# The conditioned part's weights and first x go into the first attention's memory, loaded while the last sample is still in work

## The chip, the cores and the metric

The kernel runs on one core of one Trainium2 chip. The metric is the device time of one execution in microseconds (us), lower is better. The core has five instruction queues that each work in order: PE (TensorE, matrix products and transposes; the loading of its weights is shown as PEld), DVE (VectorE), ACT (ScalarE), POOL (GpSimd) and SP (SyncE, which here only issues transfers). On-chip memory is SBUF, 128 partitions wide; products land in PSUM, which has eight banks. Inputs lie in DRAM and come in by DMA.

## The reference, cut to what matters

x has 16 samples of 256 tokens by 256 features, in float32. Four residual steps follow each other:

```python
x = x + attn0(cross_attention(x, fside, stage embedding))     # 16 heads of 16
x = x + fp4_feed_forward(x @ W[cat] + b[cat])                 # weights and rows quantized in blocks of 16
x = x + attn1(diffusion(x, zX, zY, zR))                       # 16 heads of 64, causal segments of 128
y = concat(gelu(x @ fc1.T + b1) @ fc2.T + b2,                 # 192 shared columns
           gelu(x @ fc1.T + b1) @ experts[idx].T + be[idx])   # 64 columns of the sample's own expert
x = x + SCALE * (shared_expert(y) + sum of the two best of eight experts(y), gated by softmax(y @ w_router))
```

The line that makes y is called the conditioned part here.

## The kernel before

`program` runs three things: `setup`, `woven` and `mixture`.

**woven** does the first three residual steps, one sample after another. It is a set of generators ("streams"): `stage_a` and `stage_e` (the cross attention and the first attention), `stage_f` (the quantized feed-forward), `stage_d`, `stage_p`, `stage_g` and `stage_v` (diffusion, projections, scores and values of the second attention), and some that prepare weights. `weave` asks each stream for its next operation, plans the time at which the operation could start (fixed costs per engine, 4.5 us for a transfer to land, 0.06 us for issuing one) and issues the earliest one. What it issues stands in that order on each engine (`tc.manual_schedule()`). Streams wait for each other through counters: `done["A"]` counts samples whose first attention is finished, `done["F"]` those whose feed-forward is. Samples overlap: while one is in the second attention, the next ones are in the first.

All of woven's operations carry line 162 in the profile (the helper that issues them), so they are told apart by their tiles: `wq`, `wv` and `wo` are weights of the second attention, loaded again for every group of four heads into two buffers each; `e_zT` is its normalized input; `f_ppT`, `f_oT` and `pmo` belong to its last product; `x` is the sample. When a sample is finished, `stage_v` stores it to DRAM (`xd<-x`). `stage_f` stores zeros to a DRAM table, two stores of 1 MB for each sample (`ysort<-zero`), right after the sample's feed-forward; the two of the last sample are woven's last ones.

woven's SBUF is divided into pools: `w` (weights), `x`, `sa` (all tiles of the cross attention and the first attention), `sf` (feed-forward) and `sl` (second attention). The pools are laid out one behind another and are all given back when woven ends.

**mixture** follows. Its pools lie where woven's were. It opens a PSUM pool of two times four banks (`bank0`, `bank1`), a pool `moe_keep` whose first tile is `xs` (all of x), and others, and calls `conditioned`, which loads its own weights in a pool `c2_w` (lines 1373 to 1400), then works through eight blocks of 512 tokens. A block loads the two samples' expert columns into `own` (line 1407), transposes x (line 107, then copies at line 113 into `g_xT`), and does 32 matmul instructions with `fc1` (each product of float32 data is two instructions), a gelu on ACT (line 1424), 16 with `fc2`, 32 with `own`, the router's logits and `route`, which scatters rows by indirect DMA from POOL. All matmuls of this part carry line 49, all loads of x line 1111. Unlike woven, this part is not in a written order: a list scheduler places each instruction on its engine when its own model of time finds it ready, later in the program or not. After `conditioned` come the tile plan (`plan_tiles`, line 1315 stores zeros to `osort`), four shared blocks, 35 or more tiles of the experts and the last four shared blocks.

Of the kernel before, what the change touches and what calls it, by code (L numbers as in the profile page):

```python
# [12 lines left out]
F32 = mybir.dt.float32  # L13
# [6 lines left out]
P = 128  # L20
S = 256
D = 256
# [5 lines left out]
FF1 = 1024  # L28
NE = 8
# [15 lines left out]
def mm(nc, out, pairs, start=True, stop=True):  # L45

    last = len(pairs) - 1
    for i, (lhsT, rhs) in enumerate(pairs):
        nc.tensor.matmul(out, lhsT, rhs, start=start and i == 0, stop=stop and i == last)  # L49
# [245 lines left out]
def woven(k):  # L295
    nc, tc = k.nc, k.tc
    with ExitStack() as ctx:
        g = Stages()
        g.k, g.a, g.B, g.ident = k, k.a, k.B, k.ident
        g.pe, g.dve, g.act = Unit("PE", nc.tensor), Unit("DVE", nc.vector), Unit("ACT", nc.scalar)  # L300
        g.pool, g.sp = Unit("POOL", nc.gpsimd), Unit("SP", nc.sync)
        pool = lambda name, bufs, **kw: ctx.enter_context(tc.tile_pool(name=name, bufs=bufs, **kw))
        g.w = pool("w", 1)
        g.xp = pool("x", 5)
        g.a_, g.f_, g.l_ = pool("sa", 1), pool("sf", 1), pool("sl", 1)
        space = bass.MemoryType.PSUM
        psum = pool("psum", 1, space=space)
        g.pairs = [psum.tile([P, 2, 512], F32, name=f"pair{i}") for i in range(PAIRS)]
        g.singles = [psum.tile([P, 512], F32, name=f"single{i}") for i in range(8 - 2 * PAIRS)]
        g.zT = {}  # L310
        g.live, g.kT = {}, {}
        g.x, g.io, g.done = {}, {}, {"W": 0, "D": 0, "Z": 0, "A": 0, "M": 0, "E": 0, "F": 0, "P": 0, "G": 0, "V": 0, "L": 0}
        with tc.manual_schedule():
            weave([stage_a(g), stage_e(g), stage_gate(g), stage_up(g), stage_down(g), stage_f(g), stage_g(g), stage_p(g), stage_d(g), stage_v(g), stage_fill(g)])
# [80 lines left out]
def stage_e(g):  # L395

    for b in range(g.B):
        o = g.a_.tile([P, 2, D], F32, name="b_o", tag="b_o")
        before = None
        for n in range(5):  # L400
            if n < 4:
                yield lambda: g.done["M"] > 4 * b + n
                kT, qS = g.kT.pop(4 * b + n), (yield from queries_transposed(g, n))
                prob = [(yield from heads_exponential(g, 0, kT, qS))]
            if n > 0:
                yield from heads_values(g, n - 1, before, o)
            if n < 4:
                prob.append((yield from heads_exponential(g, 2, kT, qS)))
                g.done["E"] += 1
            before = prob  # L410
        oT = g.a_.tile([P, 2, S], F32, name="b_oT", tag="b_oT")
        both = yield from single(g, o)
        pt = both.rearrange("p (c s) -> p c s", c=2)
        for c in range(2):
            for st in range(2):
                yield g.pe.transpose(pt[:, c, st * P : (st + 1) * P], o[:, st, c * P : (c + 1) * P], g.ident)
        yield copy_(g, oT, pt)
        g.singles.append(both)
        both = yield from single(g, oT)
        pp = both.rearrange("p (s d) -> p s d", s=2)  # L420
        for st in range(2):
            yield from mm_(g, pp[:, st, :], [(oT[:, c, st * P : (st + 1) * P], g.wout0[:, c, :]) for c in range(2)])
        yield g.dve.tensor_tensor(g.x[b], g.x[b], pp, ALU.add)
        g.singles.append(both)
        g.done["A"] = b + 1


def fetch_a(g, b):
# [530 lines left out]
def stage_g(g):  # L959

    for i in range(4 * g.B):
        yield lambda: g.done["P"] > i and g.done["V"] > i - 2
        g.live[i] = yield from scores4(g, i % 4, *g.live[i])
        g.done["G"] = i + 1
# [403 lines left out]
def conditioned(k, keep, r):  # L1368

    nc, tc, a = k.nc, k.tc, k.a  # L1370
    B, NT = k.B, 2 * k.B
    with ExitStack() as ctx:
        w = ctx.enter_context(tc.tile_pool(name="c2_w", bufs=1))
        p2 = ctx.enter_context(tc.tile_pool(name="c2_p2", bufs=2))

        def load(name, shape, src):
            t = w.tile(shape, F32, name=name)
            nc.sync.dma_start(out=t, in_=src)
            return t

        fc1 = load("fc1", [P, 2, FF1], a["fc1"])
        fc1b = load("fc1b", [P, 8], a["fc1b"])
        fc2 = load("fc2", [P, 8, P], a["fc2a"])
        fc2b = load("fc2b", [P, 1], a["fc2_b"][0:P].unsqueeze(1))

        wr = w.tile([P, 2, P + NE], F32, name="wr")
        nc.sync.dma_start(out=wr[:, :, P:], in_=a["w_router"])
        nc.vector.tensor_copy(wr[:, :, 0:P], k.ident.unsqueeze(1).to_broadcast([P, 2, P]))
        expb = load("expb", [16, 64], a["L1_cond2_experts_b"])

        bias2 = w.tile([P, B], F32, name="bias2")
        shared_b = load("shared_b", [64, 1], a["fc2_b"][P : P + 64].unsqueeze(1))
        nc.vector.tensor_copy(bias2[0:64, :], shared_b.to_broadcast([64, B]))
        pb = bank(k)
        mm(nc, pb[64:128, :B], [(expb, k.onehot[0:16, 2, :])])
        nc.vector.tensor_copy(bias2[64:128, :], pb[64:128, :B])
        own = []
        for i in range(3):
            t = w.tile([P, 8, P], F32, name=f"own{i}")
            nc.sync.dma_start(out=t[:, :, 0:64], in_=a["fc2c"])  # L1400
            own.append(t)

        for blk in range(NT // 4):
            k.stream = blk % 2
            for b in (2 * blk, 2 * blk + 1):
                which = nc.sync.value_load(k.idx[0:1, 2, b : b + 1], min_val=0, max_val=15)
                nc.sync.dma_start(
                    out=own[b % 3][:, :, 64:128], in_=a["exp_w"][bass.ds(which, 1)].rearrange("e p f m -> p (e f) m")
                )
                if b + 2 < B:  # L1410
                    load_x(k, b + 2)
            xT = p2.tile([P, 2, 512], F32, name="g_xT", tag="g_xT")
            transposed(
                k,
                xT.rearrange("p c (s t) -> p (c s) t", t=P),
                [k.xs[:, 4 * blk + s, c * P : (c + 1) * P] for c in range(2) for s in range(4)],
            )
            x = k.xs[:, 4 * blk : 4 * blk + 4, :]
            nc.gpsimd.tensor_tensor(x, x, k.bs2.unsqueeze(1).to_broadcast([P, 4, D]), ALU.add)
            hT = k.hp.tile([P, 8, 512], F32, name="hT", tag="hT")  # L1420
            for f in range(8):
                ph = bank(k)
                mm(nc, ph, [(fc1[:, c, f * P : (f + 1) * P], xT[:, c, :]) for c in range(2)])
                nc.scalar.activation(hT[:, f, :], ph, AF.Gelu, bias=fc1b[:, f : f + 1])
            py = bank(k)
            mm(nc, py, [(fc2[:, f, :], hT[:, f, :]) for f in range(8)])
            nc.vector.tensor_scalar(k.yT[:, 0, blk * 512 : (blk + 1) * 512], py, fc2b, None, ALU.add)
            for i in range(2):
                b = 2 * blk + i
                py = bank(k)[:, :S]  # L1430
                mm(nc, py, [(own[b % 3][:, f, :], hT[:, f, i * S : (i + 1) * S]) for f in range(8)])
                nc.vector.tensor_scalar(k.yT[:, 1, b * S : (b + 1) * S], py, bias2[:, b : b + 1], None, ALU.add)

            logits = p2.tile([P, 4, NE], F32, name="logits", tag="logits")
            part = p2.tile([P, 4, NE], F32, name="part", tag="part")
            ys = []
            for t4 in range(4):
                tok = slice(blk * 512 + t4 * P, blk * 512 + (t4 + 1) * P)
                py = bank(k)[:, : 2 * (P + NE)].rearrange("p (c w) -> p c w", c=2)
                for c in range(2):  # L1440
                    mm(nc, py[:, c, :], [(k.yT[:, c, tok], wr[:, c, :])])
                nc.vector.tensor_copy(part[:, t4, :], py[:, 1, P:])
                nc.vector.tensor_tensor(logits[:, t4, :], py[:, 0, P:], part[:, t4, :], ALU.add)
                y = p2.tile([P, 2, P], F32, name="r_y", tag="r_y", bufs=5)
                copies(k)(y, py[:, :, 0:P])
                ys.append(y.rearrange("p c d -> p (c d)"))
            route(k, r, p2, logits, ys, 4 * blk, 4)


def program(tc, a, out, n_batch):  # L1450
# [102 lines left out]
```

## Time and profile before

| what | value |
|---|---|
| median of 3 runs | 2787.61 us (2787.22 to 2788.68) |
| the profiled execution's own time | 2794.98 us |
| span of the profiled execution, first to last instruction | 2793.3 us |
| PE busy | 2701.6 us, 97% of the span |
| DVE, ACT, POOL busy | 1434.2, 934.3, 856.5 us |
| mean granted PE clock | 0.977 |
| last first-attention product on PE (`wout,b_oT`) starts | 1602.3 us |
| last feed-forward product group into x (`downT,d_hT`) starts on PE | 1667.9 us |
| woven's last PE product ends | 1799.9 us |
| first `fc1` product of the conditioned part | 1814.49 us |
| conditioned part's last router product | about 2064 us |

The profile gives times in microseconds from the span's start. A row of the timeline has the start, the length, the engine (SPq is a transfer issued by SP), the line, the operation, `out<-in` by the program's names (digits dropped: `fc` is `fc1` or `fc2`), the shape, the count, and in brackets how long the engine had been idle before and for what. A row of the windows has a stretch, its length, the busy time and count of PE, PEld, DVE, ACT and POOL, then the granted PE clock (1.00 is full speed), the share of the DMA engines in use and GB/s. A row of waits says who waited for whom: us in total, how many times, the longest.

### The profile page before, as it was taken

Reading aid. Unit: us, or ns where it says so; the run is one execution under the profiler, and the core shown is the slowest. Engines: PE = TensorE matmul, PEld = TensorE weight load, DVE = VectorE, ACT = ScalarE, POOL = GpSimd, SP = SyncE. Lnnn points to the kernel's source line nnn. Section 1 sums busy time; section 2 is a strip of 40 time slices with the busy share of each in tenths; the row PEclk is TensorE's granted clock in tenths of the full one; section 3 lists DMA queues with packets and bytes.
Section 4 is the critical chain, followed back from the end, with each engine's and each line's share of the span. In section 5 each row is a group of like instructions: output and inputs, shape, how many; then the busy total and the mean of one; then the engine's idle time right before and its main releaser. Section 6 shows DMA issues by size and latency. Waiting matters only on the chain. (4 is left out here: it accounts for less than half of the span.)

```text
span 2793.3 us, 42335 instructions
## 1 busy us (share of the span) xinstructions
PE 2701.6 (97%) x15999; PEld 2045.2 (73%) x15999; DVE 1434.2 (51%) x3113; ACT 934.3 (33%) x2418; POOL 856.5 (31%) x1030
## 2 busy tenths in 40 slices
PE   7999999999999999999999999799999999999999
PEld 5666777777777777777777778555566888888866
DVE  6456776776776776776777776433340000000023
ACT  2223334333333333333333334333222222222221
POOL 4323344434444334334434344223330000000035
PEclk7879999999999999999999999899999999999999
DMA  3122032322222222222221223241112455555523
GB/s 113 58 65 87 25 99 83 94 72 70 94 73 71 93 73 71 93 74 69 93 75 64 77 83 95 75 125 50 50 39 74 139 195 193 187 196 198 198 84 106
DMA packets 196526, 270.39 MB, mean 97 GB/s; under 512 B 34912, under 2 KB 167264, under 8 KB 186976
## 3 DMA queue, kind: packets, MB, share of 16 engines
q1 hardware_dynamic: 190176, 250.87, 28.0%
q0 software_dynamic: 6144, 16.79, 2.0%
q8 instruction: 128, 2.10, 0.3%
q14 instruction: 78, 0.64, 0.1%
HBM read 207.05 MB, written 60.56 MB: 96 GB/s over the span
## 5 line engine op out<-in xcount | busy, mean ns | idle before, releaser
L162 ACT ACTIVATE f_prob<-pair,f_stat 128x144 f32<-128x144 f32 x512 | 190.3, 377 | 225.6 <-DVE f_stat L162 171.8
L162 DVE TENSOR_TENSOR pair<-pair,mask 128x256 f32<-128x256 f32 (+1 forms) x384 | 198.4, 517 | 124.3 <-PE pair L162 93.1
L1192 POOL DMA_INDIRECT got<-osort,pos_o x64 | 62.1, 971 | 628.0 <-ACT hT L1125 585.3
L1174 ACT ACTIVATE ehT<-bank,own_b 128x256 f32<-128x256 f32 x280 | 132.5, 473 | 349.1 <-PE bank L49 349.1
L162 PE MATMUL single<-e_zT,wq 128*128 128x256 f32 x1024 | 249.3, 386 | 0.0
L49 PE MATMUL bank<-ysT,w 128*128 128x256 f32 x1120 | 247.5, 379 | 0.2 <-ACT ysT L113 0.2
L49 PE MATMUL bank<-w,ehT 128*128 128x256 f32 x1120 | 247.5, 379 | 0.0
L49 PEld LDWEIGHTS bank<-ysT,w 128*128 128x128 f32 x1120 | 212.7, 190 | 29.4 <-ACT ysT L113 0.5
L49 PEld LDWEIGHTS bank<-w,ehT 128*128 128x128 f32 x1120 | 210.2, 190 | 27.2
L162 PEld LDWEIGHTS single<-e_zT,wq 128*128 128x128 f32 x1024 | 186.8, 191 | 33.5 <-issue 4.3
L162 PE MATMUL pair<-keys,f_q 32*128 32x144 f32 x2048 | 159.8, 294 | 0.2 <-ACT f_prob L162 0.2
L162 ACT ACTIVATE b_e<-pair 128x768 f32<-128x768 f32 x128 | 103.6, 809 | 163.4 <-PE pair L162 152.8
L162 PEld LDWEIGHTS pair<-keys,f_q 32*128 32x128 f32 x2048 | 132.4, 184 | 27.7 <-issue 22.8
L162 POOL TENSOR_SCALAR_AFFINE_SELECT b_e<-b_e 128x512 f32<-128x512 f32 x128 | 83.1, 649 | 216.8 <-ACT b_e L162 216.1
L1182 DVE TENSOR_TENSOR eo<-bank,eb 128x512 f32<-128x512 f32 x35 | 24.2, 692 | 234.4 <-PE bank L49 234.4
L162 POOL TENSOR_TENSOR keys<-f_t,f_t 128x256 f32<-128x256 f32 x128 | 94.5, 751 | 150.1 <-DVE f_t L162 145.7
L162 PE MATMUL single<-wo,f_oT 128*128 128x256 f32 x512 | 130.2, 387 | 9.0 <-ACT f_oT L162 8.6
L162 DVE TENSOR_REDUCE qpad<-pair 128x2 f32<-128x256 f32 (+1 forms) x256 | 131.0, 554 | 4.4
L162 DVE TENSOR_TENSOR x<-x,single 128x512 f32<-128x512 f32 (+1 forms) x112 | 67.6, 604 | 121.3 <-PE single L162 121.2
L162 PE MATMUL pair<-b_qkT 16*128 16x128 f32 (+1 forms) x1024 | 123.0, 362 | 4.7 <-ACT b_qkT L162 3.3
L162 POOL TENSOR_TENSOR f_q<-f_t,f_t 128x256 f32<-128x256 f32 x128 | 93.4, 749 | 110.2 <-DVE f_t L162 108.3
L162 POOL TENSOR_TENSOR f_prob<-f_prob,f_stat 128x1024 f32<-128x1024 f32 x64 | 125.8, 1965 | 0.0
(294 smaller groups left out, 5255.2 us busy)
## 6 DMA issues: line engine op xcount, KB each, us to landing
w<-in_w SPq DMA_DIRECT2D x70, 1024.0 KB, 5.2
ysort<-zero SPq DMA_DIRECT2D x32, 1024.0 KB, 7.8
wq<-in_w_qk SPq DMA_DIRECT2D x128, 256.0 KB, 4.5
wv<-in_w_v SPq DMA_DIRECT2D x64, 256.0 KB, 4.3
wo<-in_w_out SPq DMA_DIRECT2D x64, 256.0 KB, 3.3
ys<-ysort SPq DMA_DIRECT2D x35, 256.0 KB, 2.7
osort<-eo SPq DMA_DIRECT2D x35, 256.0 KB, 5.4
eb<-in_b SPq DMA_DIRECT2D x35, 128.0 KB, 5.2
```

Source lines behind the costliest of these rows:

```text
L49: nc.tensor.matmul(out, lhsT, rhs, start=start and i == 0, stop=stop and i == last)
L162: return Op([(self.name, self.cost(fn, outs, aps), lambda: call(*args, **kw))], outs, aps)
L1174: nc.scalar.activation(hT[:, f, :], ph, AF.Gelu_apprx_tanh, bias=b1[:, f : f + 1])
L1182: nc.vector.tensor_tensor(o, po, b2.unsqueeze(1).to_broadcast([P, 2, D]), ALU.add)
L1192: nc.gpsimd.indirect_dma_start(out=g, out_offset=None, in_=k.osort[:, :], in_offset=bass.IndirectOffsetOnAxis(ap=r.pos_o[:, i, t : t + 1], ...
```

## The change

The pool `sa` is opened on the other side of SBUF, so that it can be given back by itself. At the end of `stage_e`, when all samples' feed-forwards are done, it is given back, and a new function `fetch_c` opens the conditioned part's weight pool in its place and issues 11 loads there as operations of that stream: two halves of the first block's x (from `xd`), `fc1`, `fc1b`, `fc2`, `fc2b`, the router's weights, the experts' bias, the shared bias, and the shared columns of two `own` buffers. It also makes the tiles `bias2` and `xT0`, which no load fills. `conditioned` no longer loads these; it takes the tiles from `k.early`. There are two `own` buffers instead of three. The transposed x has one buffer in the block's pool and the early tile `xT0`, used in turn. The first block's transposes read the early `x0`; `xs` is still loaded for all samples and is still what the residual is added to.

```diff
-        g.a_, g.f_, g.l_ = pool("sa", 1), pool("sf", 1), pool("sl", 1)
+        g.f_, g.l_ = pool("sf", 1), pool("sl", 1)
+
+        g.attention0 = tc.tile_pool(name="sa", bufs=1, side="right")
+        g.a_ = g.attention0.__enter__()
...
         g.done["A"] = b + 1
+    yield lambda: g.done["F"] == g.B
+    g.attention0.__exit__(None, None, None)
+    yield from fetch_c(g)
+
+
+def fetch_c(g):
+
+    k, a = g.k, g.a
+    k.c2 = k.tc.tile_pool(name="c2_w", bufs=1, side="right")
+    w = k.c2.__enter__()
+    k.early = {}
+
+    def get(name, shape, src=None):
+        k.early[name] = t = w.tile(shape, F32, name=name)
+        if src is not None:
+            yield g.sp.dma_start(out=t, in_=src)
+
+    yield from get("x0", [P, 4, D])
+    for b in range(2):
+        yield g.sp.dma_start(out=k.early["x0"][:, 2 * b : 2 * b + 2, :], in_=k.xd[b].rearrange("(s p) d -> p s d", p=P))
+    yield from get("fc1", [P, 2, FF1], a["fc1"])
+    yield from get("fc1b", [P, 8], a["fc1b"])
+    yield from get("fc2", [P, 8, P], a["fc2a"])
+    yield from get("fc2b", [P, 1], a["fc2_b"][0:P].unsqueeze(1))
+    yield from get("wr", [P, 2, P + NE])
+    yield g.sp.dma_start(out=k.early["wr"][:, :, P:], in_=a["w_router"])
+    yield from get("expb", [16, 64], a["L1_cond2_experts_b"])
+    yield from get("shared_b", [64, 1], a["fc2_b"][P : P + 64].unsqueeze(1))
+    for i in range(2):
+        yield from get(f"own{i}", [P, 8, P])
+        yield g.sp.dma_start(out=k.early[f"own{i}"][:, :, 0:64], in_=a["fc2c"])
+    yield from get("bias2", [P, g.B])
+    yield from get("xT0", [P, 2, 512])
...
-        own = []
-        for i in range(3):
-            t = w.tile([P, 8, P], F32, name=f"own{i}")
-            nc.sync.dma_start(out=t[:, :, 0:64], in_=a["fc2c"])
-            own.append(t)
...
-                    out=own[b % 3][:, :, 64:128], in_=a["exp_w"][bass.ds(which, 1)].rearrange("e p f m -> p (e f) m")
+                    out=own[b % 2][:, :, 64:128], in_=a["exp_w"][bass.ds(which, 1)].rearrange("e p f m -> p (e f) m")
...
-            xT = p2.tile([P, 2, 512], F32, name="g_xT", tag="g_xT")
+            xT = p2.tile([P, 2, 512], F32, name="g_xT", tag="g_xT", bufs=1) if blk % 2 else k.early["xT0"]
+            xs = k.xs[:, 4 * blk : 4 * blk + 4, :] if blk else k.early["x0"]
             transposed(
                 k,
                 xT.rearrange("p c (s t) -> p (c s) t", t=P),
-                [k.xs[:, 4 * blk + s, c * P : (c + 1) * P] for c in range(2) for s in range(4)],
+                [xs[:, s, c * P : (c + 1) * P] for c in range(2) for s in range(4)],
             )
```

More of the change, by code (lines that the diff above doesn't have):

```diff
@@ L1372, in conditioned @@
     with ExitStack() as ctx:
-        w = ctx.enter_context(tc.tile_pool(name="c2_w", bufs=1))
         p2 = ctx.enter_context(tc.tile_pool(name="c2_p2", bufs=2))
[L1376 to L1387, printed above, removed]
+        fc1, fc1b, fc2, fc2b, wr = (k.early[n] for n in ("fc1", "fc1b", "fc2", "fc2b", "wr"))
+        own = [k.early[f"own{i}"] for i in range(2)]
         nc.vector.tensor_copy(wr[:, :, 0:P], k.ident.unsqueeze(1).to_broadcast([P, 2, P]))
[L1389 to L1393, printed above, removed]
+        bias2 = k.early["bias2"]
+        nc.vector.tensor_copy(bias2[0:64, :], k.early["shared_b"].to_broadcast([64, B]))
         pb = bank(k)
-        mm(nc, pb[64:128, :B], [(expb, k.onehot[0:16, 2, :])])
+        mm(nc, pb[64:128, :B], [(k.early["expb"], k.onehot[0:16, 2, :])])
         nc.vector.tensor_copy(bias2[64:128, :], pb[64:128, :B])
-        own = []
-        for i in range(3):
-            t = w.tile([P, 8, P], F32, name=f"own{i}")
-            nc.sync.dma_start(out=t[:, :, 0:64], in_=a["fc2c"])
-            own.append(t)
         for blk in range(NT // 4):
@@ L1430, in conditioned @@
                 py = bank(k)[:, :S]
-                mm(nc, py, [(own[b % 3][:, f, :], hT[:, f, i * S : (i + 1) * S]) for f in range(8)])
+                mm(nc, py, [(own[b % 2][:, f, :], hT[:, f, i * S : (i + 1) * S]) for f in range(8)])
                 nc.vector.tensor_scalar(k.yT[:, 1, b * S : (b + 1) * S], py, bias2[:, b : b + 1], None, ALU.add)
@@ L1447, in conditioned @@
             route(k, r, p2, logits, ys, 4 * blk, 4)
+    k.c2.__exit__(None, None, None)
 def program(tc, a, out, n_batch):
```

## The prediction

> **What bounds the kernel now.** I read the page's slices first, then the timeline around the one dip that the change can touch, then the waits of that stretch and the clock by windows.
>
> The page's second part cuts the span into 40 slices of 69.8 us; a digit is a tenth busy.
>
> ```profile
> PE   7999999999999999999999999799999999999999
> ...
> PEclk7879999999999999999999999899999999999999
> ```
>
> PE is at 9 in all slices but the first and the 26th (1745 to 1815 us). PE sets the time: an edit counts only as far as it removes PE idle time or half-clock time, or adds some. The 26th slice holds the hand-over from the woven part to the mixture. Its timeline:
>
> ```profile
> 1799.31 0.59 PE L162 MATMUL single<-pmo,f_ppT 128*128 128x256 f32 x2
> 1800.01 0.69 DVE L162 TENSOR_TENSOR x<-x,single 128x512 f32<-128x512 f32 x1 [2.62 <-PE single L162]
> 1800.04 0.33 SPq L1378 DMA_DIRECT2D fc<-in_fc  x1
> ...
> 1800.72 0.38 SPq L162 DMA_DIRECT2D xd<-x  x1
> ...
> 1806.04 0.89 SPq L1111 DMA_DIRECT2D xs<-xd  x2
> ...
> 1812.29 0.36 PE L49 MATMUL bank<-onehot,expb 16*64 16x16 f32 x2 [12.38 <-DMA expb<-in_L_cond_experts_b]
> ...
> 1812.58 1.97 PE L107 MATMUL bank<-ident,xs 128*128 128x128 f32 x8
> ...
> 1814.49 15.39 PE L49 MATMUL bank<-g_xT,fc 128*128 128x512 f32 x32
> ```
>
> PE's last woven product ends at 1799.90. It then stands 12.4 us, by the brackets for the load of `expb`. That name is only the last of a row: `fc1` is issued at 1800.04 because its pool lies on tiles that PE read until 1799.90, and SP then sits at the load of `xs`, which the waits explain:
>
> ```profile
> SPq L1111 <- DMA xd<-x: 3.6, 1, 3.6
> ```
>
> `xs` lies where woven's pools were and waits for the last sample's store to land; the small loads stand behind it on SP. So the gap is: memory free, a queue of loads, landing. The idle also costs clock:
>
> ```profile
> 1800.00:1803.00 3.00, 0.00 (x0) 0.00 (x0) 0.89 (x2) 0.00 (x0) 0.00 (x0) 1.00 0.65 137
> ...
> 1804.00:1812.00 8.00, 0.00 (x0) 0.00 (x0) 0.57 (x3) 0.00 (x0) 1.13 (x14) 0.50 0.73 216
> 1812.00:1817.00 5.00, 4.71 (x13) 3.03 (x14) 1.04 (x3) 1.87 (x2) 2.34 (x1) 0.50 1.10 209
> ```
>
> The granted clock (the column before the last two) is still 1.00 until 1803, 0.50 from 1804, and remains 0.50 for the first 5 us of the new work.
>
> **The change part by part.**
>
> *The hand-over, removed.* With weights, biases and the first x in memory, what holds block 0's transposes is PSUM. I take it that a new pool waits for the whole old pool under it, because `xs`, the first tile of its pool, waits for a store of x, which lies elsewhere in that area. The last reader of woven's PSUM is the DVE addition that ends at 1800.70. Then on PE: 0.05 for the hand-over between engines; the bias product, 0.29 (1812.29 to 1812.58); from the first transpose to the first `fc1` product 1.44 at full clock (block 1: transposes at 1845.34, `fc1` at 1846.78, rows below). `fc1` starts at 1800.70 + 0.05 + 0.29 + 1.44 = 1802.48 instead of 1814.49: **12.0 us**.
>
> *The clock.* PE's pause would be 0.9 us, plus about 0.4 for the copy of the transposed x, against 3 us that the clock stayed up in the row 1800 to 1803. So block 0's `fc1` runs at full clock. Before, it took 1829.71 - 1814.49 = 15.22 until the first `fc2` product. At full clock block 1 shows it, with 0.31 of `route` between (1852.89 to 1853.20):
>
> ```profile
> 1845.34 1.04 PE L107 MATMUL bank<-ident,xs 128*128 128x128 f32 x8
> 1846.78 6.28 PE L49 MATMUL bank<-g_xT,fc 128*128 128x512 f32 x14 [0.41 <-ACT g_xT L113]
> ...
> 1853.20 7.97 PE L49 MATMUL bank<-g_xT,fc 128*128 128x512 f32 x18
> 1861.01 7.03 PE L49 MATMUL bank<-hT,fc 128*128 128x512 f32 x16
> ```
>
> 1861.01 - 1846.78 - 0.31 = 13.92, so **1.3 us** more. [...]
>
> *The eleven loads, moved.* They go on SP where the stream issues them: after the last sample's feed-forward, so behind its two zero stores and ahead of the next `wq`:
>
> ```profile
> 1661.36 1.31 SPq L162 DMA_DIRECT2D ysort<-zero  x2
> ...
> 1662.71 3.69 SPq L162 DMA_DIRECT2D wq<-in_w_qk  x2
> ...
> 1666.44 1.41 SPq L162 DMA_DIRECT2D wv<-in_w_v  x1
> ```
>
> Their own memory is long free (last reader of `sa`: PE, `wout,b_oT`, 1602), so SP doesn't wait at them. Issuing costs SP about 5.4 us (0.33 to 0.8 each, rows of 1800 to 1813), which nothing needs. Their bytes do matter, as the queue is served in order (`xd`, behind `fc1`, took 5.3 us to land against a median of 3.3). They are 0.52 MB of x, 1.57 MB of `fc1` and `fc2`, 0.52 MB of `own`. x at 360 GB/s (what the zero stores and `wq` ran at, 1664 to 1668): 1.5 us. `fc1` and `fc2` at 400 (a mean of 1803 to 1806): 3.9. Each `own` 1.16, by the lone `exp_w` load in the same 256-byte pieces (1841.5 to 1842.7). Small ones 0.5. Sum 8.2 us. That `wq` landed at 1662.71 + 8.6 = 1671.3 and would land at 1679.5. Its user:
>
> ```profile
> 1680.84 1.99 PE L162 MATMUL single<-e_zT,wq 128*128 128x256 f32 x8
> ```
>
> So 1.3 us remain: **no stall**. From both sides: at 370 GB/s throughout 7.1 us, slack 2.4; at the 272 GB/s of 1801 to 1810 (2.45 MB in 9 us) 9.6 us, a stall of 0.1. The list scheduler may also bring block 0's two `exp_w` loads forward, whose memory is now free. It did so with a store of much later code:
>
> ```profile
> 40.91 2.27 SPq L1315 DMA_DIRECT2D osort<-zero  x4
> ```
>
> If they land before `wq`, 2.3 us more: a stall of up to 2.4. Behind `wv`, they meet the `wo` issued at 1679.33 and used at 1689.0: landing by about 1686, hidden. I take 0; PE is full there, so any stall would count whole.
>
> *The planner.* 11 x 0.06 = 0.66 us more on SP in its plan; the moved `wq` would be planned about 15 us ahead of its use, so the order of the other engines should stay. 0.
>
> *Two `own` instead of three; one `g_xT` and `xT0`.* `own` of block 1 can be loaded when block 0's products with it end (1840.1 and 1843.6 before), lands 3.3 later, and is used at 1867.87: 21 us of cover by the `fc1` and `fc2` products. If SP were held up longer than that, each excess microsecond would count in all seven blocks. The transposed x has two buffers as before. The third `own` load (256 KB) goes. All 0.
>
> *What is late next.* `xs` for block 0 now only feeds the residual on POOL; for block 1 it is loaded when `xd` lands (now 2.9 to 3.3 us after 1800.7, without `fc1` ahead) and is needed at about 1832. `hT` needs memory that PE leaves at 1799.9. Gelu's table load (1.28) falls into the first 1.7 us product. 0.
>
> **Sum**: 12.0 + 1.3 - 0 = 13.3 us off the profiled execution, 2794.98 to 2781.7. That execution is 7.4 us above the median of the runs, a distance the change doesn't touch; on the median 2787.61 - 13.3 = **2774.3 us**.
>
> **Rivals.** *A, another gate takes over* (15 in 100): the transposes or the gelu wait for `xd` landing after all, as `xs` does, or the scheduler puts a copy behind something of POOL that waits for it. `xd` lands at about 1803.8, the clock drops in the pause: 3 to 5 us of the gain go, 2777 to 2779.5. For it: POOL's first instructions waited the same way, until 1806.21. Against: nothing the first block reads or writes lies there.
>
> *B, late weights in the drain* (10): the burst takes longer than 9.5 us; 2 to 5 us of stall, 2776 to 2780.
>
> *C, more than the gap* (12): if PSUM is given tile by tile, the banks of `pair` are free by 1789.2 and the bias product, transposes and some `fc1` products fall into the idle of 1789 to 1797, also lifting the clock there; up to 3 of idle and 2.5 of half clock: 2768.5 to 2771.5. Against: the wait of `xs`.
>
> *D, the gain is eaten* (7): A and B at their worst, 2782 to 2793.
>
> *E, slower* (6): the burst starves the second attention's weights. Place: the products with `wq` at 1680.84. Price: each microsecond by which the burst exceeds 9.5 us is a PE stall, and later `wq`, `wv` and `wo` come behind it. The change turns to a loss when the burst costs 9.5 + 13.3 = 22.8 us, past 0.2% at 28.4: 2793.5 or more. That is 2.6 MB at 92 GB/s; the 1 MB loads of this trace land in 5.2 us at the median.
>
> **How the numbers follow.** My case has 50 in 100, 2772 to 2776. About 0.2% (5.6 us) is what a measurement of this kernel can tell from no change: 2782.0 and 2793.2 are the borders. Faster: 50 + 15 + 10 + 12 = 87; same 7; slower 6. The range 2769 to 2780.5 leaves out D, E and a fifth of C.
>
> **What would show it.** In the changed profile the loads of `fc1` stand right behind the last zero stores near 1663; the `wq` product near 1680.8 has no idle before it, or the idle is B; the first transposes follow the last addition into x within 0.1 us; the clock stays at 1.00 through block 0; first `fc2` product at about 1816.4. Wrong if the bias product waits for a store or if PE's order changes before 1799.

## The result and the profile after

The changed kernel takes **2774.41 us** (median of 6 runs, 2773.11 to 2776.45) against 2788.17 for the kernel before beside it; the ratio is 0.9948, with a 95% interval of 0.9938 to 0.9959. The prediction was 2774.3. In later runs, beside three of the experiments, the changed kernel had 2775.78 against 2789.89, ratio 0.9947 (0.9934 to 0.9961). The profiled execution took 2774.55 us, its span is 2772.9.

The slices of the page (now 69.3 us each) still have a dip in PE at the hand-over, one digit less deep, and the clock row has no dip there any more:

```profile
PE   7999999999999999999999999899999999999999
...
PEclk7989999999999999999999999999999999999999
```

The timeline of the changed kernel through the hand-over follows, with PE's rows and one of DVE (start, length, engine, line, operation; idle before it in brackets). Its first rows are the *drain*: the last operations of woven's last sample, from the transposes of its last probabilities (`f_prob`) on.

```profile
1784.78 1.97 PE L162 MATMUL single<-ident,f_prob 128*128 128x128 f32 x8 [5.06 <-POOL f_prob L162]
...
1789.82 2.08 PE L162 MATMUL single<-wo,f_oT 128*128 128x256 f32 x4
1791.68 1.06 PE L162 MATMUL single<-pmo,f_ppT 128*128 128x256 f32 x2
...
1794.19 0.59 PE L162 MATMUL single<-pmo,f_ppT 128*128 128x256 f32 x2
1794.89 0.69 DVE L162 TENSOR_TENSOR x<-x,single 128x512 f32<-128x512 f32 x1 [4.74 <-PE single L162]
1795.64 0.28 PE L49 MATMUL bank<-onehot,expb 16*64 16x16 f32 x2 [0.85 <-DVE x L162]
1795.85 1.09 PE L107 MATMUL bank<-ident,x 128*128 128x128 f32 x8
1797.23 14.00 PE L49 MATMUL bank<-xT,fc 128*128 128x512 f32 x32 [0.28 <-ACT xT L113]
1811.07 7.03 PE L49 MATMUL bank<-hT,fc 128*128 128x512 f32 x16
```

The 12.38 us of waiting for `expb` have become 0.85 us of waiting for the last addition into x. PE's last woven product ends at 1794.19 + 0.59 = 1794.78 and `fc1` starts 2.45 us later; before, these lay 1814.49 - 1799.90 = 14.59 apart. The first `fc2` product comes 13.84 us after the first `fc1` product; before it was 15.22.

The same stretch by windows (length, then busy time and count of PE, PEld, DVE, ACT and POOL, granted clock, DMA share, GB/s):

```profile
1784.00:1788.00 4.00, 3.07 (x16) 2.34 (x18) 0.69 (x1) 0.59 (x1) 0.72 (x1) 0.50 0.00 0
1788.00:1794.00 6.00, 5.88 (x24) 4.34 (x21) 0.42 (x1) 0.59 (x1) 0.00 (x0) 0.50 0.01 3
1794.00:1796.00 2.00, 1.15 (x7) 0.68 (x6) 0.69 (x1) 0.00 (x0) 0.00 (x0) 0.97 0.00 0
1796.00:1800.00 4.00, 3.72 (x15) 2.04 (x15) 1.14 (x4) 1.30 (x2) 1.13 (x14) 1.00 0.41 124
1800.00:1812.00 12.00, 12.00 (x30) 5.30 (x29) 0.29 (x1) 5.95 (x9) 2.35 (x1) 1.00 1.00 306
```

The clock is 1.00 through block 0. In the drain ahead of it, it is 0.50 for longer than before. There the transposes of `f_prob` began at 1792.01 and the clock was up again at about 1797, some 5 us later:

```profile
1792.01 1.97 PE L162 MATMUL single<-ident,f_prob 128*128 128x128 f32 x8 [5.05 <-POOL f_prob L162]
...
1795.00:1797.20 2.20, 2.08 (x15) 1.35 (x14) 0.24 (x1) 0.58 (x1) 0.00 (x0) 0.58 0.00 0
1797.20:1799.90 2.70, 2.70 (x12) 2.04 (x12) 0.19 (x1) 0.00 (x0) 0.00 (x0) 1.00 0.00 0
```

Here it takes about 9 us, from 1784.78 to 1794.1. That is the part of the result that the prediction did not have.

The burst of loads in SP's timeline, and the product on PE that needs the next `wq`:

```profile
1654.03 1.31 SPq L162 DMA_DIRECT2D ysort<-zero  x2
1655.38 3.88 SPq L162 DMA_DIRECT2D x<-xd  x2
1659.31 1.36 SPq L162 DMA_DIRECT2D fc<-in_fc  x1
...
1665.43 3.30 SPq L162 DMA_DIRECT2D own<-in_fc2c  x2
1668.78 1.49 SPq L162 DMA_DIRECT2D wq<-in_w_qk  x2
...
1673.52 1.99 PE L162 MATMUL single<-e_zT,wq 128*128 128x256 f32 x8
```

It stands where it was expected, behind the last zero stores, and the product with `wq` at 1673.52 has no idle before it.

**Where to measure.** The spans differ by 20.4 us, more than the change is worth, so the two traces are compared by stretches that begin at the same instruction. The last zero stores (`ysort`) are a good mark, as PE is almost full from there to the drain. Three stretches follow: from these stores to the transposes of `f_prob` after the drain's 5-us idle; from there to the first `fc2` product; from there to the end. The two profiles of each kernel (us; all but the first column are differences of two starts in that kernel's timeline, and "end" is the end of the span):

| kernel | first zero stores at | last zero stores to `f_prob` | `f_prob` to first `fc2` | first `fc2` to end |
|---|---|---|---|---|
| before | 168.97 | 130.65 | 37.70 | 963.6 |
| before, profiled again | 168.79 | 130.66 | 37.48 | 963.6 |
| after | 163.33 | 130.75 | 26.29 | 961.8 |
| after, profiled again | 163.99 | 130.75 | 24.85 | 961.8 |

So of the 20.4 us in the first pair, 7.3 lie ahead of the last zero stores (1661.36 and 1654.03), where the two kernels do the same; 11.4 at the hand-over; 1.8 in the tail; and the burst costs 0.1.

### The profile page after: what moved, and what is told of

The parts are those of the page before. It is cut to its first block, busy times and chain, and to the rows that moved or that the text cites. A ratio compares the mean times of both kernels' runs of the same rounds, so it can differ in the third digit from the quotient of the medians.

```text
span 2772.9 us, 42339 instructions
## 1 busy us (share of the span) xinstructions
PE 2692.8 (97%) x15999; PEld 2039.9 (74%) x15999; DVE 1434.2 (52%) x3113; ACT 935.5 (34%) x2418; POOL 858.2 (31%) x1030
```

## The experiments

In each, "whole change" means the changed kernel, and the diff shown is against it unless said otherwise.

**Layout without early loads.** The tiles and the two `own` buffers stay, but the pool is opened by `conditioned` on memory that woven's last sample still uses, and x is read from `xs`.

```diff
...
-    yield lambda: g.done["F"] == g.B
-    g.attention0.__exit__(None, None, None)
-    yield from fetch_c(g)
...
-    k.c2 = k.tc.tile_pool(name="c2_w", bufs=1, side="right")
+    k.c2 = k.tc.tile_pool(name="c2_w", bufs=1)
...
     with ExitStack() as ctx:
+        fetch_c(k)
...
-            xs = k.xs[:, 4 * blk : 4 * blk + 4, :] if blk else k.early["x0"]
+            xs = k.xs[:, 4 * blk : 4 * blk + 4, :]
```

> All of the change but its purpose: the first attention's pool on the other side, two own buffers, the second transposed x in the weight pool; but that pool is opened in the conditioned part, where woven's second-attention tiles were, its loads are issued there, and block 0 reads xs as before. Theory (the gain is the early loads and the clock that follows, the rest costs and brings nothing): the gap is back, 2786.5 to 2789.5 us, first fc1 product 13 to 15 us after woven's last product. Rival (part of the gain comes from the layout or from the smaller buffers): below 2784.

Measured 2790.72 us against 2787.66, ratio 1.0005 (0.9994 to 1.0016); that is 1.2 above the expected range, and no gain. PE's timeline is that of the kernel before, with the same wait:

```profile
1812.25 0.36 PE L49 MATMUL bank<-onehot,expb 16*64 16x16 f32 x2 [12.40 <-DMA expb<-in_L_cond_experts_b]
1812.54 1.97 PE L107 MATMUL bank<-ident,xs 128*128 128x128 f32 x8
```

`f_prob` to first `fc2` is 37.60. So the gain comes from the early loads; of two `own` buffers and the alternating transposed x no cost and no gain can be measured.

**Weights early, x late.**

```diff
-    yield from get("x0", [P, 4, D])
-    for b in range(2):
-        yield g.sp.dma_start(out=k.early["x0"][:, 2 * b : 2 * b + 2, :], in_=k.xd[b].rearrange("(s p) d -> p s d", p=P))
...
-            xs = k.xs[:, 4 * blk : 4 * blk + 4, :] if blk else k.early["x0"]
+            xs = k.xs[:, 4 * blk : 4 * blk + 4, :]
```

> The changed kernel without the early x: weights and tables are loaded early, block 0's transposes read xs, which can only be loaded when the last sample's store has landed (2.2 us after its issue in the changed profile). Theory: transposes start at the store's landing plus a load's landing, 2.2 + 3 to 4 us later than with x0, and the pause of some 6 us drops the clock again (1.8 us): 5.5 + 1.8, about 7 us above the changed kernel, 2780 to 2783. Rival (only the weights matter): 2774 to 2776. Rival (only x matters): 2786 or more.

Measured 2782.93 us, ratio 0.9975 (0.9968 to 0.9982). The timeline shows what remains when only the weights are there:

```profile
1800.03 0.38 SPq L162 DMA_DIRECT2D xd<-x  x1
1800.05 0.28 PE L49 MATMUL bank<-onehot,expb 16*64 16x16 f32 x2 [0.85 <-DVE x L162]
1802.30 0.89 SPq L1144 DMA_DIRECT2D xs<-xd  x2
1805.26 2.02 PE L107 MATMUL bank<-ident,xs 128*128 128x128 f32 x8 [4.93 <-issue]
```

The bias product is on time; `xs` is issued 2.3 us after the last sample's store and PE stands another 4.93 us, after which it is at half clock (8 transposes in 2.02 instead of 1.09; the granted clock is 0.53 from 1805 to 1810). From the last zero stores to the first `fc2` product this kernel has 162.72 us, against 168.35 in the kernel before and 157.04 and 155.60 in the changed kernel: about half of the gain needs x, the other half the weights alone bring.

**Three more 1 MB stores in the burst.** They stand between the eleven loads and the next `wq`, and write zeros over rows of `osort` that get zeros anyway.

```diff
         yield g.sp.dma_start(out=k.early[f"own{i}"][:, :, 0:64], in_=a["fc2c"])
+    for i in range(3):
+        rows = k.osort[i * 8 * P : (i + 1) * 8 * P, :].rearrange("(p r) d -> p r d", p=P)
+        yield g.sp.dma_start(out=rows, in_=k.zero.unsqueeze(1).to_broadcast([P, 8, D]))
```

> The changed kernel with three more stores of 1 MB zeros (to rows of osort that are overwritten later) between the eleven loads and the next wq. Theory: at some 350 GB/s they take 9.0 us in the queue; the wq had about 1.4 us to spare in the changed profile, so PE stalls about 7.5 us at the first product with that wq, and the stall counts whole: 2780.5 to 2783. Rival (the drain has slack, transfers ahead of wq are hidden anyway): 2774 to 2776.

Measured 2785.27 us, ratio 0.9988 (0.9978 to 0.9997): 2 to 5 us more than expected. The wait is where it was expected, at the products with `wq`:

```profile
1671.80 4.02 SPq L162 DMA_DIRECT2D osort<-zero  x3
1675.86 3.91 SPq L162 DMA_DIRECT2D wq<-in_w_qk  x2
...
1685.06 3.62 PE L162 MATMUL single<-e_zT,wq 128*128 128x256 f32 x8 [8.45 <-DMA wq<-in_w_qk]
```

The idle is 8.45 us, 1 more than the 7.5 I had taken; if the stores took the 9.0 us of the expectation, only some 0.5 us had been to spare (an estimate). The rest of the miss is the clock. By windows (columns as above):

```profile
1682.00:1684.00 2.00, 0.00 (x0) 0.00 (x0) 0.00 (x0) 0.00 (x0) 0.00 (x0) 0.50 0.95 216
1684.00:1686.00 2.00, 0.94 (x2) 0.84 (x3) 0.00 (x0) 0.00 (x0) 0.00 (x0) 0.50 1.09 370
1686.00:1688.00 2.00, 2.00 (x6) 1.57 (x5) 0.00 (x0) 0.00 (x0) 0.00 (x0) 0.50 1.01 328
```

The group that waited takes 3.62 instead of 1.99 us, 1.63 more. Last zero stores to `f_prob`: 140.87 against 130.75, so 10.12 = 8.45 + 1.63 + 0.04. Nothing of it is absorbed later. This is the rival "slower" made real: 3 MB more in the queue eat ten of the thirteen microseconds.

**The pool in the same place, the loads written in `conditioned`.** The pool lies where `sa` was, but no stream issues the loads; the list scheduler places them.

```diff
...
-    yield lambda: g.done["F"] == g.B
-    g.attention0.__exit__(None, None, None)
-    yield from fetch_c(g)
...
     with ExitStack() as ctx:
+        fetch_c(k)
...
```

> The memory of the change without its stream: the weight pool lies where the first attention's was, but the loads are written in the conditioned part, and the list scheduler may place them. Theory (memory is what held the loads back; the scheduler brings ready loads forward): they are issued well before the hand-over, behind or between woven's own, first transposes within 0.2 us of the last addition into x, 2773 to 2776. Rival (the loads must be in the stream): they stand at the end, 2783 to 2788.

Measured 2775.65 us, ratio 0.9956 (0.9942 to 0.9970), which can't be told from the whole change. SP's timeline:

```profile
1598.60 0.90 SPq L444 DMA_DIRECT2D x<-xd  x2
1599.54 0.47 SPq L440 DMA_DIRECT2D fc<-in_fc  x1
1600.21 0.55 SPq L162 DMA_DIRECT2D wv<-in_w_v  x1
...
1608.91 1.89 SPq L1422 DMA_DIRECT2D own<-in_exp_w  x2
```

The loads floated some 60 us further forward than the stream puts them (the first is issued 58.6 us ahead of the last zero stores, in the changed kernel 1.4 behind them), in between woven's own, right to where PE's last reader of `sa` lets go of their memory (SP waits 4.0 us for that ahead of the first of them). Where the tiles lie is what counts; the stream and its place in the order are not needed.

**Woven's and the mixture's PSUM in two pools each.** Whole change, plus:

```diff
-    return k.ps.tile([P, 512], F32, name=f"bank{k.stream}", tag=f"bank{k.stream}")
+    return k.ps[k.stream].tile([P, 512], F32, name=f"bank{k.stream}", tag=f"bank{k.stream}")
...
-        psum = pool("psum", 1, space=space)
+        psum = pool("psp", 1, space=space)
         g.pairs = [psum.tile([P, 2, 512], F32, name=f"pair{i}") for i in range(PAIRS)]
+        psum = pool("pss", 1, space=space)
         g.singles = [psum.tile([P, 512], F32, name=f"single{i}") for i in range(8 - 2 * PAIRS)]
...
-        k.ps = ctx.enter_context(tc.tile_pool(name="ps", bufs=4, space=bass.MemoryType.PSUM))
+        k.ps = [ctx.enter_context(tc.tile_pool(name=f"ps{i}", bufs=4, space=bass.MemoryType.PSUM)) for i in range(2)]
```

> The whole change, with the on-chip product memory (PSUM) of the woven part held in two pools (the pairs of banks, the single banks) and that of the mixture in two pools of four banks as well. My theory: a new pool waits for the whole old pool under it, so in the changed kernel the last addition into x is the gate of everything on PE. With two pools the half that lies on the pairs is free when the last scores are exponentiated, and PE can fill its 5 us of idle in the last sample's drain with block 0's bias product, transposes and first products, which also keeps the clock up: 2767 to 2771 us, 5 to 7 us below the changed kernel. Rival (memory is given out tile by tile already, so the pool is not what holds the banks; or the scheduler can't reach past the written order of the woven part): 2773 to 2776, no difference.

Measured **2767.85 us** (5 runs, 2767.24 to 2771.51), ratio to before 0.9927 (0.9913 to 0.9940). The changed kernel beside it has 2771.71 to 2776.87: the ranges don't meet. This version beats both kernels. PE's timeline:

```profile
1782.39 0.28 PE L49 MATMUL bank<-onehot,expb 16*64 16x16 f32 x2 [2.48 <-ACT f_prob L162]
1782.60 1.09 PE L107 MATMUL bank<-ident,x 128*128 128x128 f32 x8
1783.97 1.98 PE L49 MATMUL bank<-xT,fc 128*128 128x512 f32 x2 [0.28 <-ACT xT L113]
1785.75 1.91 PE L162 MATMUL single<-ident,f_prob 128*128 128x128 f32 x8
1787.45 1.06 PE L49 MATMUL bank<-xT,fc 128*128 128x512 f32 x2
...
1792.76 0.59 PE L162 MATMUL single<-pmo,f_ppT 128*128 128x256 f32 x2
1793.19 11.32 PE L49 MATMUL bank<-xT,fc 128*128 128x512 f32 x26
1804.35 7.03 PE L49 MATMUL bank<-hT,fc 128*128 128x512 f32 x16
```

Block 0's bias product now waits for the exponential that reads the last pair of banks, not for the addition into x, and half the drain's idle, the pauses in the last products and the 0.85 us are filled with work that has to be done anyway. Last zero stores to first `fc2`: 1804.35 - 1654.22 = 150.13, against 130.75 + 26.29 = 157.04 and 155.60 in the two profiles of the changed kernel.

**Fillers in the drain.** Whole change, plus products of the identity with itself, which nobody reads, wherever PE would wait between the last scores and the end of woven:

```diff
...
+def stage_fill_end(g):
+
+    yield lambda: g.done["G"] == 4 * g.B
+    one = g.singles.pop()
+    while g.done["V"] < 4 * g.B:
+        op = g.pe.matmul(one[:, :P], g.ident, g.ident, start=True, stop=True)
+        op.filler = True
+        yield op
+    g.singles.append(one)
```

> The whole change, with some 16 products of the identity with itself put into the woven part's order for PE between the last scores and the last probabilities, into a bank that nothing reads. They compute nothing that is used. They test whether the part of the gain that is missing against my sum (1.9 us) and the half-clock stretch before the hand-over are the clock alone: if the clock rises again because PE is busy, the drain's last products run at full clock, 2 to 3 us less, 2771 to 2773 us. Rival (the clock follows the heat or power of the heavy part before, not the idle): 2774 to 2776, no difference, or slower by the fillers' own time.

Measured 2772.5 us (2770.85 to 2776.5), ratio 0.9943 (0.9929 to 0.9956): by the medians 3.3 less than the changed kernel beside it, but the ranges overlap, so the times alone don't settle it. PE's timeline does; the granted clock is 1.00 in each 2-us window from 1778 to 1804:

```profile
1780.42 3.39 PE L162 MATMUL single<-ident 128*128 128x128 f32 x28 [0.78 <-DVE x L162]
1784.70 1.09 PE L162 MATMUL single<-ident,f_prob 128*128 128x128 f32 x8 [0.89 <-POOL f_prob L162]
...
1788.19 1.13 PE L162 MATMUL single<-wo,f_oT 128*128 128x256 f32 x4 [0.37 <-ACT f_oT L162]
```

The transposes of `f_prob` take 1.09 instead of 1.97, and from their start to the end of the last woven product it is 6.34 us. In the changed kernel's two profiles that is 10.00 and 8.57, in the kernel before 7.89 twice. Last zero stores to first `fc2`: 153.36, so 2.2 to 3.7 less. What the drain lost was the clock: PE waits for the same inputs, and only its idle is filled.

**Both together.** The diffs of the last two kernels in one:

```diff
...
+        psum = pool("pss", 1, space=space)
...
+def stage_fill_end(g):
...
```

> The two preceding edits together: two PSUM pools, and the products that fill the drain's idle. If the pools let real work into the idle, the fillers stand in its way and add nothing: 2767 to 2771. If the pools do nothing, the result is that of the fillers alone: 2771 to 2773, or 2774 to 2776 if neither does anything.

Measured 2771.67 us (2767.65 to 2772.62), ratio 0.9932 (0.9918 to 0.9945); last zero stores to first `fc2` 151.44. The median is just above the 2767 to 2771 that I had expected, the ranges of this kernel and of the two pools alone overlap, and in the trace it is 1.3 worse than those: the planner puts 28 filler instructions where block 0's products would have gone, and block 0's `fc1` starts only after woven's last product.

**The two PSUM pools on the kernel before.** The diff is against the kernel before.

```diff
...
-        psum = pool("psum", 1, space=space)
+        psum = pool("psp", 1, space=space)
...
+        psum = pool("pss", 1, space=space)
...
-        k.ps = ctx.enter_context(tc.tile_pool(name="ps", bufs=4, space=bass.MemoryType.PSUM))
+        k.ps = [ctx.enter_context(tc.tile_pool(name=f"ps{i}", bufs=4, space=bass.MemoryType.PSUM)) for i in range(2)]
```

> The kernel before with the two PSUM pools alone, without the early loads. My theory: before, the loads of x and the weights are the gate, so banks that come free earlier have nothing to work on; from the last zero stores of the woven part to the first fc2 product 168 us as in the kernel before, ratio 0.998 to 1.002. Rival: the two pools are worth their 6 us by themselves, ratio 0.998 or less.

Measured 2787.44 us against 2789.25, ratio 0.9995 (0.9984 to 1.0006): nothing. PE's timeline:

```profile
1788.92 0.59 PE L162 MATMUL single<-pmo,f_ppT 128*128 128x256 f32 x2
1802.07 0.36 PE L49 MATMUL bank<-onehot,expb 16*64 16x16 f32 x2 [12.56 <-DMA expb<-in_L_cond_experts_b]
```

So PSUM becomes the gate only once the loads are early.

**Before and after, profiled again.** 

> The changed kernel as it is, beside the three others on the same chip: 2774.4 us as before, the measure for each of them.

> The kernel before as it is, profiled once more, to tell what of its own first profile was chance: the first zero stores of the woven part came at 169.0 us there and at 163.3 to 168.6 in the other kernels, and the end came 963.6 us after the first fc2 product there and 961.7 in most others. My theory: both differences are the phase of the granted clock and differ between executions of one kernel; from the last zero stores to the first fc2 product 168 to 170 us again. Rival: the change itself moves the beginning or the tail; then this profile repeats 169.0 and 963.6.

Measured 2775.78 and 2789.53 us; their rows are in the table above. From `f_prob` to the first `fc2` product the changed kernel differs by 1.44 us between its two profiles, of which 1.43 is the drain's clock (10.00 and 8.57 us from `f_prob` to the end of woven's last product); the kernel before differs by 0.22. The kernel before repeated 168.79 and 963.6, which by itself would fit the rival; the other kernels decide. The kernel before with two PSUM pools does the same work in woven and has its first zero stores at 157.24; so the beginning is not set by the change. Of the tail's 1.8 us, 1.7 are one group of products with `w1s` after an idle of 1.97 us, which all kernels have. The first row is of the kernel before, the second of the changed kernel:

```profile
2676.52 15.67 PE L49 MATMUL bank<-yT,w1s 128*128 128x512 f32 x32 [1.97 <-DVEq L1098]
...
2657.84 13.97 PE L49 MATMUL bank<-yT,w1s 128*128 128x512 f32 x32 [1.97 <-DVEq L1134]
```

It took 15.67 in four of the twelve profiles: twice in the kernel before, in the layout without early loads, and in the kernel with fillers, which has the early loads. The kernel before with two pools has 13.97. The change does not set it either.

## Why the prediction was right, and where not

- **The hand-over removed (12.0): right, 12.14.** The gap from the last woven product to `fc1` went from 14.59 to 2.45, in both profiles of the changed kernel. The gate is the one named: the bias product follows the last addition into x (1794.89 + 0.69 = 1795.58) by 0.06 us. That it is PSUM that holds the transposes, and that a new pool waits for all of the old one, was an inference; splitting the pools moved the gate to the last reader of the pairs, so it is shown.
- **The clock in block 0 (1.3): right, 1.38.** `fc1` took 13.84 instead of 15.22. With the quicker transposes (1.91 from the first transpose to `fc1` before, 1.38 now) half clock had cost 1.38 + 0.53 = 1.91 us there. The rows of before give 1.3 + 0.47 = 1.8 for the two (0.47 is 1.91 less the 1.44 of block 1), the 1.8 in the expectation for the kernel with x late. The short pauses ahead of `fc1` (0.85 and 0.28 us) did not lower the clock: it is 1.00 from 1794.13 to the end of block 0's `fc1` in the first profile, and in each 2-us window from 1795 to 1807 in the second. In the first of them full clock had been back for only 0.65 us when woven's last product ended; in the kernel before it was 3.07 (1796.83 to 1799.90).
- **The eleven loads (no stall): right in the sum, thin, and wrong in two of its steps.** No idle stands before the products with `wq`. But issuing the eleven was not 5.4 us of SP's time: from 1655.38 to the next `wq` at 1668.78 it is 13.4, with 3.88 for the two halves of x alone and 3.30 for the two `own`. For 2.5 us of this SP waited for earlier loads of the burst to land (in its waits from 1650 to 1690, 1.8 for `fc` and 0.7 for x). So `wq` is issued only 4.74 us before its use: the burst delays the issuing as well as the bytes. And the `exp_w` loads did float, but not to where I had looked: to 1595.59, before the burst, where SP waits for them. In the view of SP's waits from 1590 to 1610 (us in total, times, longest):

```profile
SPq L1425 <- PE single L162: 3.9, 1, 3.9
```

SP stood 3.9 us until PE's last reader of `sa` was done, with a `wv` load (issued at 1597.14) behind it; no PE idle follows. My value of 0 survives, though the case for it was weaker than I made it. One reading in it was wrong: the median of 3.3 us for `xd` mixes in the loads of `xs`; the 16 stores alone land in 2.2, so 5.3 behind `fc1` was the longer delay, which favours the order of the queue that I argued for.
- **What was left out: the drain's clock.** The sum assumed that nothing before 1799.9 changes. The two confirmed terms are 12.14 + 1.38 = 13.5, yet `f_prob` to first `fc2` fell by 37.70 - 26.29 = 11.4 in the first pair of profiles and by 37.48 - 24.85 = 12.6 in the second. The difference is the last woven products at half clock for longer: 10.00 and 8.57 us against 7.89. In the kernel with the loads placed by the scheduler, the same hand-over has 7.49, less than before. So it varies between executions, 7.5 to 10.0, and a sum from one profile can't contain it; the range did. The forecast put the first `fc2` product 155.0 us behind the last zero stores (1816.4 - 1661.36); it came 157.0 and 155.6 behind them. That the medians fell by 13.8 and 14.1 agrees with 13.5, but that 2774.41 lies within 0.2 of the forecast is luck: the drain alone moves it by more.
- **The planner's order, two `own`, what is late next: right at 0.** The stretch from the last zero stores to `f_prob` (130.65 to 130.75) shows the first, the layout without early loads the second; and PE's timeline of the changed kernel has no idle above 0.41 us from `fc1` to the `fc2` products of block 1 at 1842.37.
- **Rivals.** A: POOL's first instruction does wait for the store of x (13.16 us idle, until 1797.89), but nothing on PE waits for it. B and E: the mechanism exists, as the three stores show, and its price is the stall that was described and 1.63 us of half clock on top; the burst of the change is just short enough. C did not happen, for the reason given against it; the two-pool kernel is rival C built on purpose, and its 2767.85 is just below the 2768.5 to 2771.5 put down for it.

## What to carry to other kernels

When an engine stands at a hand-over between two parts, look for what makes the first load wait: here it was memory that the old part's last sample holds, and a tile moved to memory that came free earlier let the scheduler bring its load forward by itself. After that ask what the next gate is; here it was a PSUM pool given back as a whole, worth another 8 us by the medians and 5.5 to 6.9 in the traces for four lines, and worth nothing before the loads were moved. Bytes added to a queue ahead of a load in use counted almost in full here (8.45 us of stall for stores estimated at 9.0), and with the idle came 1.63 us of half clock on top.

## What the runs showed of the hardware beyond that

The same sequence after the same idle of 5.05 or 5.06 us took a different time in different executions: from the transposes of `f_prob` to the end of woven's last product 7.49, 7.50, 7.89 (three times), 7.90, 8.57, 8.60 and 10.00 us in nine profiles, and 6.34 with the idle filled. After an idle of 1.97 us, the same in twelve profiles, the products with `w1s` took 15.67 us in four and 13.97 in eight: 1.70 lost, or nothing.

The granted clock of the traces shows what differs. In the kernel before, the idle of 1.97 us lasts from 2674.55 to 2676.52; the clock is 1.00 until 2677.47 and 0.50 from there to 2680.88, for 3.41 us, as the last column but two shows:

```profile
2677.00:2679.00 2.00, 2.00 (x4) 0.82 (x3) 0.00 (x0) 0.00 (x0) 0.00 (x0) 0.62 0.06 12
2679.00:2681.00 2.00, 2.00 (x4) 0.83 (x3) 0.00 (x0) 0.69 (x1) 0.48 (x1) 0.53 0.00 0
```

In the changed kernel the idle lasts from 2655.87 to 2657.84, and the clock is 1.00 from 2640 to 2680. In the drain half clock lasts 10.24 us in the first profile of the changed kernel (1783.89 to 1794.13) and 6.83 in the first of the kernel before (1790.01 to 1796.83). From the windows I estimate about 6.8 us in the second profile of the changed kernel (0.79 from 1787 to 1789, 0.50 up to 1795, then 1.00), and 3.4 in the kernel with the loads placed by the scheduler, whose drain took 7.49 (0.78 from 1785 to 1790, 0.88 from 1790 to 1795). What decides after which of these idles the clock falls, and how long it stays down, was not shown; nor was the phase that the last expectation takes for it.

In the changed kernel with two PSUM pools, where block 0's products fill part of the drain, the clock was 0.53 from 1784 to 1786, 0.62 from 1786 to 1788 and 1.00 from 1788. In the changed kernel's first profile, where PE pauses between groups, it was 0.50 in every 2-us window from 1784 to 1794. The beginning of woven, where PE is partly idle (in the kernel before it is busy for 10.35 of the first 20 us), differs by up to 12 us between profiles (first zero stores at 157.24 to 168.97). From 60 to 80 us the granted clock was 0.50 in the slowest of these and 0.96 in the quickest, so it differs there too; no run was made for that alone.
